# Down products of two feed-forward blocks by seven block products, with the block sums on GpSimd

## The chip, the cores and the metric

The kernel runs on one core of a Trainium2 chip. The metric is the device time of one launch in microseconds (us). The engines are TensorE (PE: matmuls, and PEld: its weight loads), VectorE (DVE), ScalarE (ACT), GpSimd (POOL) and SyncE (SP), which issues the DMAs. Each engine takes its instructions in the order in which they stand in its own queue and waits at semaphores for the others.

## What is computed

Two transformer layers over x of 4 batches x 256 positions x 256 features, all in f32:

```python
x = x + _L0_attn_ref(_layernorm(x), q_kernel, kv_kernel, out_kernel, q_norm_scale, k_norm_scale)
x = x + _L0_ffn_ref(_layernorm(x), w_gate, w_up, w_down)
x = x + _L1_attn_ref(_layernorm(x), W_K, W_Q, W_V, W_O)
x = x + _L1_ffn_ref(_layernorm(x), W1, W2, W3)
```

The change touches the two feed-forward blocks, here FFN0 and FFN1:

```python
# FFN0 (hidden size 1024)
h = silu(x @ w_gate) * (x @ w_up)
h_sparse = h * mask          # of each four neighbours the two largest by absolute value
out = h_sparse @ w_down      # 1024 -> 256
# FFN1 (hidden size 1024)
hidden = fwht(silu(x @ W1.T) * (x @ W3.T))   # Walsh-Hadamard transform along the hidden axis
out = hidden @ W2.T                          # 1024 -> 256
```

## The kernel before

**Stages.** The kernel runs attention 0 (`attention0`), FFN0 (`ffn0`), attention 1 (`attention1`) and FFN1 (`ffn1`). x stays in SBUF for the whole time, as eight tiles `xs` of 128 positions x 256 features, two per batch. A tile framework orders the instructions: it takes the program as written, estimates when each instruction could run and fixes an order for each engine when the program is built. Buffers come from pools of tagged tiles; a tag with n buffers hands them out in turn, and who gets one waits for the readers of the tile that had it before. `page` is a tag of eight 4 KB pages; the pool `late` (attention 1 and both FFNs) has the tags `qk` (2 buffers), `v` (3) and `u` (4), among others.

**FFN0.** The loop `for n in range(8)` goes over batch b = n // 2 and half gc = n % 2 of the hidden features. One step does this:
- `gated`: for w_gate, then w_up, 8 matmuls of 128x256 into a PSUM tile `pgu` (two such tiles exist: one for gate, one for up, reused in each step). ScalarE makes s = silu(gate), VectorE h = up * s (L557).
- ScalarE makes a = |h| (L530), and VectorE keeps two of four in h (`keep_two_of_four`: three comparisons at L569, 8 small sums in bf16 at L581 and L582, 4 products at L583). The positions are arranged so that the four neighbours lie in four different planes of h.
- `normed(.., by_dma=True)` at some steps: the layer norm of a later batch, whose transposition goes over a GpSimd copy (`xpl`, L240), a DMA and a ScalarE copy (`xnT`, L195).
- For n >= 2, `down(hs, n - 2, down_sb)`: the down product of two steps before, 2 position tiles x 4 matmuls of 128x256 into two PSUM tiles `po_f`. When the second half of a batch has been added, VectorE adds each `po_f` to `xs` (L604).

The down products of n = 6 and 7 are left for `finish_ffn0`, which attention 1 calls in its first step.

**Attention 1.** A software pipeline of project, score and attend over 16 units (head group, batch). Its projections use seven block products instead of eight already (`seven_products`, with sums of blocks from `left_of` for activations and `right_of` for weights, on VectorE). A unit's scores are exponentiated on ScalarE (L226), scaled on GpSimd (`p`, L234), split into 16-bit planes on GpSimd (`pl`, L240), transposed by DMA (`plT`), joined again by VectorE and ScalarE copies (`pT`, L260) and multiplied with the values on TensorE (`av`). Towards its end the Hadamard transform is applied to the weights W2 instead of to the hidden features: matmuls with a 128x128 Hadamard matrix, then 12 GpSimd additions and subtractions of 128x512 (L830).

**FFN1.** Again 8 steps; `gated1` makes gate and up of one half by `seven_products` and h from them (L873 on ScalarE, L874 on VectorE). Into the gaps between its products it pulls pieces of the iterator `between`, here the down product of the step before, `down(hs, n - 1, w2h[0], last=True)`, which adds to `xs` and sends finished rows of the output by DMA.

Of the kernel before, what the change touches and what calls it, by code (L numbers as in the profile page):

```python
# [11 lines left out]


# [1 line left out]

# [5 lines left out]
F32 = mybir.dt.float32  # L21
# [3 lines left out]
ALU = mybir.AluOpType  # L25
AX = mybir.AxisListType

P = 128
B, T, D = 4, 256, 256
NT = T // P  # L30
# [18 lines left out]
def two_layers(ctx, tc, consts, tables, x, wq, wkv, wo, w_gate, w_up, w_down,  # L49
               w_k, w_q, w_v, w_o, w1, w3, w2, out):  # L50
    nc = tc.nc
# [21 lines left out]
    def wide(name):  # L73
        return ps2.tile([P, 2, 512], F32, tag="wide", name=name)

    def bank(shape, name):
        return ps1.tile([P, *shape], F32, tag="bank", name=name)

    def page(name):

        return work.tile([P, 4, T], F32, tag="page", name=name, bufs=8)
# [11 lines left out]
    xs = [xpool.tile([P, D], F32, tag=f"x{t}", name=f"x{t}") for t in range(B * NT)]  # L93
# [11 lines left out]
    def load_ffn(src, shape, name):  # L105
        t = fpool.tile([P, *shape], F32, tag="fw", name=name)
        nc.sync.dma_start(t, src)
        return t
# [21 lines left out]
    down_sb = load_ffn(w_down, (NF, D), "w_down")  # L130
# [392 lines left out]

    def ffn0():
        hs, xn = {}, dict(enumerate(xn_f))
        for n in range(8):
            b, gc = divmod(n, 2)
            hs[n] = h = gated(xn[b], gate_sb, up_sb, 4 * gc, "h")
            a = page("a")
            nc.scalar.activation(a, h, AF.Abs)  # L530
            keep_two_of_four(a, h)
            if gc == 0 and b + 2 < B:
                xn[b + 2] = normed(b + 2, by_dma=True)
            if n >= 2:
                run(down(hs, n - 2, down_sb))
            if n == 4:
                xn1[0] = normed(0, by_dma=True)
            if n == 6:
                xn1[1] = normed(1, by_dma=True)
                left1[0] = left_of(xn1[0])  # L540
        return lambda: run(*(down(hs, n, down_sb) for n in (6, 7)))

    def gated(xnT, w_g, w_u, f0, name):

        ps = []
        for w in (w_g, w_u):
            o = wide("pgu").rearrange("p two (f t) -> p (two f) t", t=T)
            for j in range(4):
                for c in range(NC):
                    nc.tensor.matmul(  # L550
                        o[:, j, :], lhsT=w[:, c, f0 + j, :], rhs=xnT[:, c, :],
                        start=(c == 0), stop=(c == NC - 1),
                    )
            ps.append(o)
        s, h = page("s"), page(name)
        nc.scalar.activation(s, ps[0], AF.Silu)
        nc.vector.tensor_tensor(h, ps[1], s, ALU.mult)  # L557
        return h

    def keep_two_of_four(a, h):  # L560

        c = []
        counts = work.tile([P, 8, T], BF16, tag="page", name="counts", bufs=8)
        for i in range(3):
            n = 3 - i
            ci = counts[:, (0, 3, 5)[i] : (3, 5, 6)[i], :]
            nc.vector.tensor_tensor(  # L569
                ci, a[:, i : i + 1, :].to_broadcast([P, n, T]), a[:, i + 1 :, :], ALU.is_ge  # L570
            )
            c.append({i + 1 + k: ci[:, k, :] for k in range(n)})
        sums = (
            (c[0][1], ALU.add, c[0][2], ALU.add, c[0][3], 2.0, ALU.is_ge),
            (c[1][2], ALU.add, c[1][3], ALU.subtract, c[0][1], 1.0, ALU.is_ge),
            (c[2][3], ALU.subtract, c[0][2], ALU.subtract, c[1][2], 0.0, ALU.is_ge),
            (c[0][3], ALU.add, c[1][3], ALU.add, c[2][3], 1.0, ALU.is_le),
        )
        for j, (u, op0, v, op1, w, bound, keep) in enumerate(sums):
            n = counts[:, 6 + j % 2, :]  # L580
            nc.vector.tensor_tensor(n, u, v, op0)  # L581
            nc.vector.tensor_tensor(n, n, w, op1)  # L582
            nc.vector.scalar_tensor_tensor(h[:, j, :], n, bound, h[:, j, :], keep, ALU.mult)  # L583
# [3 lines left out]
    def down(hs, n, w, last=False):  # L587


        b, gc = divmod(n, 2)  # L590
        if gc == 0:
            pos[b] = [bank([D], "po_f") for _ in range(NT)]
        for t in range(NT):
            for j in range(4):
                nc.tensor.matmul(  # L595
                    pos[b][t], lhsT=hs[n][:, j, t * P : (t + 1) * P],
                    rhs=w[:, 4 * gc + j, :], start=(gc == 0 and j == 0),
                    stop=(gc == 1 and j == 3),
                )
                if j == 1:  # L600
                    yield
            if gc == 1:
                x = xs[b * NT + t]
                nc.vector.tensor_tensor(x, pos[b][t], x, ALU.add)  # L604
                if last:
                    at = (b * NT + t) * P
                    nc.sync.dma_start(out[at : at + P, :], x)
            yield

    def run(*generators):  # L610
        for g in generators:
            for _ in g:
                pass
# [9 lines left out]
    def left_of(xnT):  # L623

        s = late.tile([P, 4, P], F32, tag="xs4", name="xs4", bufs=4)
        x11, x12, x21, x22 = (xnT[:, c, t * P : (t + 1) * P] for t in range(2) for c in range(2))
        for i, a, b, op in (
            (0, x21, x22, ALU.add), (1, s[:, 0], x11, ALU.subtract),
            (2, x11, x21, ALU.subtract), (3, x12, s[:, 1], ALU.subtract),
        ):  # L630
            nc.vector.tensor_tensor(s[:, i], a, b, op)
        return x11, x12, s[:, 3], x22, s[:, 0], s[:, 1], s[:, 2]

    def right_of(w11, w12, w21, w22, t):

        for i, a, b, op in (
            (0, w12, w11, ALU.subtract), (1, w22, t[0], ALU.subtract),
            (2, w22, w12, ALU.subtract), (3, w21, t[1], ALU.subtract),
        ):
            nc.vector.tensor_tensor(t[i], a, b, op)  # L640
        return w11, w21, w22, t[3], t[0], t[1], t[2]

    def seven_products(product, x, z, y, c11, c12, c21, c22, shape, z_alone=True):
# [208 lines left out]
    def gated1(x, r, last, between):  # L852

        def product(o, i, first):
            for j in range(4):
                nc.tensor.matmul(  # L858
                    o[:, j, :], lhsT=r[j // 2][i - 1][:, j % 2, :], rhs=x[i - 1],
                    start=(first and j == 0), stop=True, skip_group_check=True,  # L860
                )

        gu = late.tile([P, 2, 4, T], F32, tag="qk", name="gu")
        c = gu.rearrange("p k (a m) (t c) -> p (k a) m t c", m=2, t=NT)
        for i, _ in enumerate(seven_products(
            product, st([P, 4, P], "gu_x"), bank([4, P], "gu_z"), st([P, 4, P], "gu_y"),
            *(c[:, :, m, t, :] for t in range(2) for m in range(2)), [P, 4, P],
        )):
            for _ in range({3: 1, 5: 2}.get(i, 0)):
                next(between, None)  # L870
        s, h = page("s"), page("h1")
        for t in (slice(0, P), slice(P, T)) if last else (slice(0, T),):
            nc.scalar.activation(s[:, :, t], gu[:, 0, :, t], AF.Silu)  # L873
            nc.vector.tensor_tensor(h[:, :, t], gu[:, 1, :, t], s[:, :, t], ALU.mult)  # L874
        return h

    def ffn1():
        hs, left = {}, {0: left_of(xn_f[0])}
        for n in range(9):
            if n < 8:  # L880
                b, half = divmod(n, 2)
                before = down(hs, n - 1, w2h[0], last=True) if n else iter(())
                hs[n] = gated1(left[b], r_ffn1[half], n == 7, before)
                run(before)
                if n == 0:
                    xn = {1: normed(1)}
                if half == 1 and b + 2 < B:
                    xn[b + 2] = normed(b + 2, by_dma=True)
                if half == 0 and b + 1 < B:
                    left[b + 1] = left_of(xn[b + 1])  # L890
            else:
                run(down(hs, n - 1, w2h[0], last=True))

    xn_f, xn1, left1, w2h, r_ffn1 = [], {}, {}, [], []
# [5 lines left out]
    late = ctx.enter_context(  # L900
        tc.tile_pool(name="late", bufs=2, reuse_waits="tile", side="right")
    )
    load_group1(0)
    load_group1(1)

    finish_ffn0 = ffn0()
    xn_f.clear()
    ps2_open.close()
    w1_sb = load_ffn(w1, (NC, NF, P), "w1")
    w3_sb = load_ffn(w3, (NC, NF, P), "w3")  # L910
    w2_raw = load_ffn(w2, (NF, D), "w2")
    st_open, st_pool = open_pool("st", bufs=4, space=PSUM)
    attention1(finish_ffn0)
    ffn1()
    st_open.close()

# [81 lines left out]
```

## Time and profile before

Three runs took 738.60, 738.98 and 739.04 us, a median of 738.98. The profiled execution has a span of 737.2 us; the traces' times are counted from the start of that span. The page gives no other time of that execution; what a run holds around its span is the 1.8 us between the two.

| stretch of the profiled execution, us | what runs | PE busy | DVE busy | ACT busy | POOL busy |
|---|---|---|---|---|---|
| 0 to 278.8 | attention 0 | 271.24 | 215.66 | 192.44 | 204.57 |
| 278.8 to 371.7 | FFN0 and the first projection of attention 1 | 92.47 | 71.94 | 25.92 | 11.17 |
| 371.7 to 655.0 | attention 1 | 282.11 | 146.33 | 157.30 | 125.51 |
| 655.0 to 737.2 | FFN1 | 79.17 | 35.21 | 31.27 | 3.79 |

How to read the profile: busy time is the union of an engine's instructions in a stretch. An instruction's row has its source line (L557), its engine, what it writes and reads, the shape of one instruction, and how often. Matmuls overlap in a pipeline: the time between the starts of two is their pace, while the length of one (0.38 us for 128x256) also holds its way through the array. A matmul of f32 in the code shows as two records. A timeline row is: start, length from the first start to the last end of the group, engine, line, operation, how often, and in brackets the engine's idle time just before it with what ended it. Another view gives all instructions of one line, with the shortest, median and longest in ns.

### The profile page before, as it was taken

To read this page: it belongs to the slowest core of one execution; us is meant where nothing else is said; L and a number is where in the kernel's file an instruction comes from. 1 tells how busy PE (TensorE), PEld (TensorE's weight loads), DVE (VectorE), ACT (ScalarE), POOL (GpSimd) and SP (SyncE) were. 2 spreads that over 40 slices of the span, in tenths; PEclk is the share of its full clock that TensorE was granted. 3 is DMA by queue.
4 is the path that set the end of the run, shared out by engine and by line. 5 is a ranking of instruction groups with operands and counts; after the bars stand their busy time and mean duration, and the time that the engine had idled before them with its cause. 6 is when DMAs were issued, how large, how long until landed. Compare 5 with 4: busy or idle time off the path is not lost.

```text
span 737.2 us, 11593 instructions
## 1 busy us (share of the span) xinstructions
PE 725.0 (98%) x3912; PEld 594.6 (81%) x3912; DVE 469.2 (64%) x1402; ACT 406.9 (55%) x983; POOL 345.0 (47%) x489
## 2 busy tenths in 40 slices
PE   9999999999999999999999999999999999999998
PEld 5556576666666778888898999999998999899997
DVE  6999878888887537987655644464442655464443
ACT  2487887667767952222355555555556576434332
POOL 1588878897799631011116433343336575520000
PEclk9999999999999999999999999999999999999999
DMA  8732344425445545001324532342232223401100
GB/s 327 293 64 51 57 93 81 92 52 93 90 79 96 77 114 180 16 14 26 119 72 77 127 55 44 70 129 46 44 72 44 44 44 44 88 15 22 23 14 30
DMA packets 138348, 57.51 MB, mean 78 GB/s; under 512 B 131504, under 2 KB 133680, under 8 KB 137520
## 3 DMA queue, kind: packets, MB, share of 16 engines
q1 hardware_dynamic: 138288, 56.77, 33.9%
q8 instruction: 31, 0.51, 0.3%
q14 instruction: 29, 0.24, 0.1%
HBM read 22.94 MB, written 1.05 MB: 33 GB/s over the span
## 4 chain that ended last, share of the span: by engine, by line
PE 75%; DVE 9%; POOL 7%; issue 4%; ACT 3%; DMA 2%; SPq 0%; POOLq 0%; DVEq 0%; ACTq 0%
PE pj L446 10%; PE pgu L550 7%; PE po L292 7%; PE po_f L595 7%; PE qk_x L783 5%; PE po L280 5%; PE sc L214 5%; PE gu_x L858 4%; PE av L394 3%; PE qk_y L783 3%; PE v_x L789 3%; PE sc L213 3%; PE av L268 2%; POOL p L234 2%; PE gu_y L858 2%
## 5 line engine op out<-in xcount | busy, mean ns | idle before, releaser
L234 POOL TENSOR_SCALAR p<-p,rs 128x128 f32<-128x128 f32 (+1 forms) x256 | 115.4, 470 | 153.2 <-DVE rs L231 147.9
L240 POOL TENSOR_SCALAR pl<-p 128x1536 uint16<-128x1536 uint16 x64 | 94.3, 1474 | 4.8 <-POOL p L234 0.5
L260 ACT COPY pT<-plT 128x1536 uint16<-128x1536 uint16 (+1 forms) x60 | 86.2, 1494 | 11.5 <-DMA plT<-pl 11.5
L216 DVE CUSTOM_DVE_ANT_0 p<-sc,cst 128x128 f32<-128x128 f32 (+1 forms) x256 | 79.7, 351 | 10.5 <-PE sc L214 8.1
L226 ACT ACTIVATE p<-p,nb,r 128x128 f32<-128x128 f32 (+1 forms) x128 | 68.2, 535 | 20.2 <-DVE nb L223 20.2
L446 PE MATMUL pj<-wq,xnT 128*128 128x512 f32 x128 | 61.1, 595 | 1.1 <-DVE qT L508 1.1
L446 PE MATMUL pj<-wkv,xnT 128*128 128x512 f32 x128 | 60.1, 592 | 0.0
L226 ACT ACTIVATE p<-p,nb 128x128 f32<-128x128 f32 (+1 forms) x128 | 56.3, 447 | 4.0 <-DVE nb L221 4.0
L292 PE MATMUL po<-wo,zT 128*128 128x256 f32 x256 | 57.9, 379 | 0.0
L280 PE MATMUL po<-w_o,zT 128*128 128x256 f32 x256 | 57.6, 379 | 0.0
L456 ACT ACTIVATE sq<-pj 128x512 f32<-128x512 f32 (+1 forms) x64 | 30.9, 489 | 42.7 <-DVE qc L451 42.4
L292 PEld LDWEIGHTS po<-wo,zT 128*128 128x128 f32 x256 | 48.3, 190 | 7.0 <-ACT kT L519 0.6
L280 PEld LDWEIGHTS po<-w_o,zT 128*128 128x128 f32 x256 | 47.7, 190 | 6.0
L156 POOL TENSOR_SCALAR ve<-mv 128x2 f32<-128x2 f32 (+1 forms) x17 | 4.3, 253 | 97.5 <-DVE mv L152 97.0
L446 PEld LDWEIGHTS pj<-wkv,xnT 128*128 128x128 f32 x128 | 24.3, 190 | 30.2 <-issue 28.0
L451 DVE TENSOR_TENSOR qs<-pj,sin_s 128x512 f32<-128x512 f32 (+1 forms) x64 | 35.3, 551 | 13.5 <-PE pj L446 12.9
L446 PEld LDWEIGHTS pj<-wq,xnT 128*128 128x128 f32 x128 | 23.5, 190 | 24.2 <-issue 19.9
L666 ACT COPY qk<-qk_x 128x512 f32<-128x512 f32 x16 | 9.4, 587 | 58.1 <-PE qk_x L783 58.1
L268 PE MATMUL av<-pT,v 128*128 128x256 f32 x128 | 38.4, 382 | 1.2 <-DVE nb L221 1.1
L214 PE MATMUL sc<-kT,qT 128*128 128x256 f32 x128 | 38.3, 381 | 0.0
L214 PE MATMUL sc<-qk 128*128 128x256 f32 x128 | 38.2, 380 | 0.0
L240 POOL TENSOR_SCALAR qpl<-qc 128x1024 uint16<-128x1024 uint16 x20 | 28.8, 1453 | 18.9 <-PE av L398 8.2
(151 smaller groups left out, 1748.8 us busy)
## 6 DMA issues: line engine op xcount, KB each, us to landing
w<-in_w_dram SPq DMA_DIRECT2D x3, 1024.0 KB, 4.7
wq<-in_wq_dram SPq DMA_DIRECT2D x4, 512.0 KB, 7.6
wkv<-in_wkv_dram SPq DMA_DIRECT2D x4, 512.0 KB, 8.4
wo<-in_wo_dram SPq DMA_DIRECT2D x4, 512.0 KB, 10.2
w_qk<-in_w_q_dram SPq DMA_DIRECT2D x4, 512.0 KB, 5.2
w_qk<-in_w_k_dram SPq DMA_DIRECT2D x4, 512.0 KB, 6.1
w_v<-in_w_v_dram SPq DMA_DIRECT2D x4, 512.0 KB, 7.3
w_o<-in_w_o_dram SPq DMA_DIRECT2D x4, 512.0 KB, 6.0
```

The lines of the kernel that those rows point to most:

```text
L214: nc.tensor.matmul(sc[:, P : 3 * P], lhsT=q[:, P:T], rhs=k, start=True, stop=True)
L216: last_of["mx"] = nc.vector.tensor_tensor_reduce(out=p[:, j, cols], in0=sc[:, cols], in1=mask[:, cols], scale=1.0, scalar=-3.0e38, op0=ALU ...
L226: last_of["exp"] = nc.scalar.activation(p[:, j, cols], p[:, j, cols], AF.Exp, bias=nb[:, j, i : i + 1], scale=SCALE1 if rq is None else rq ...
L234: nc.gpsimd.tensor_scalar(p[:, j, cols], p[:, j, cols], rs[:, j, i : i + 1], 1.0, ALU.mult, ALU.mult)
L240: last_of["planes"] = nc.gpsimd.tensor_scalar(o, i, 1.0, 1.0, ALU.mult, ALU.mult)
L260: copy(words.rearrange("p (n w) -> p w n", w=2), halves[:, :, js].rearrange("p w j n -> p w (j n)"),)
L268: nc.tensor.matmul(av, lhsT=v0, rhs=pT[:, 0:T], start=True, stop=False, skip_group_check=True)
L280: nc.tensor.matmul(po[:, t, :], lhsT=zT[:, j, t * P : (t + 1) * P], rhs=w[:, j, :], start=(t == j == 0), stop=(j == 3), skip_group_check=True,
L292: nc.tensor.matmul(po, lhsT=zTs[hd // 4][:, hd % 4, t * P : (t + 1) * P], rhs=w[:, hd, :], start=(hd == 0), stop=(hd == n - 1),)
L446: last_of[0] = nc.tensor.matmul(pj, lhsT=xnT[:, c, t * P : (t + 1) * P], rhs=w[:, g, c, :], start=(c == 0), stop=(c == NC - 1),)
L550: nc.tensor.matmul(o[:, j, :], lhsT=w[:, c, f0 + j, :], rhs=xnT[:, c, :], start=(c == 0), stop=(c == NC - 1),)
L783: last_of[1] = nc.tensor.matmul(o[:, j, :], lhsT=wqk[i - 1][:, j // 2, j % 2, :], rhs=x[i - 1], start=(first and j == 0), stop=True, skip_ ...
```

## The change

In both FFNs the down products of the first three batches are made by seven block products instead of eight; the fourth batch keeps `down`. For one batch, h is cut into two tiles of positions and two halves of hidden features, the weights into two halves of hidden features and two of output features. Four sums of blocks of h (`left_of_down`) and four of the weights (`right_of_down`), each 128x512 f32, are made on GpSimd. `down_by_seven` has three 128x128 slices x, y and z of one PSUM tile `po_s`. Each product is 4 matmuls of 128x128 into a slice; after each, VectorE adds the slice to a quarter of the batch's rows of `xs` (L658 after the change). x serves for products 1, 6, 7 and 4 in turn, accumulating, y for 5 and 3, z for 2.

In FFN0 a batch's seven products are made a batch later: four of them in the second step of the next batch and three in the step after (all seven of batch 2 in step 7). In FFN1 they are pulled between the products of the next batch's two steps, and step 7 also pulls the first half of the last batch's down product. The weights' sums of FFN0 take a buffer of tag `qk`, those of FFN1 the space of the raw W2. The sums of h take buffers of `u` or `qk` in FFN0 and of `v` in FFN1; a and s of FFN0 move from `page` to `v`.

```diff
     def ffn0():
         hs, xn = {}, dict(enumerate(xn_f))
+        blocks = late.tile([P, 4, 4, P], F32, tag="qk", name="down_t")
+        right = right_of_down(down_sb, [blocks[:, i] for i in range(4)])
+        left, by_seven = {}, {}
         for n in range(8):
             b, gc = divmod(n, 2)
             hs[n] = h = gated(xn[b], gate_sb, up_sb, 4 * gc, "h")
-            a = page("a")
+            a = late.tile([P, 4, T], F32, tag="v", name="a", bufs=3)
             nc.scalar.activation(a, h, AF.Abs)
             keep_two_of_four(a, h)
             if gc == 0 and b + 2 < B:
                 xn[b + 2] = normed(b + 2, by_dma=True)
-            if n >= 2:
-                run(down(hs, n - 2, down_sb))
+            if gc == 1 and b + 1 < B:
...
+                left[b] = left_of_down(hs[n - 1], hs[n], s)
+            if gc == 1 and b >= 1:
+                by_seven[b - 1] = down_by_seven(left[b - 1], right, b - 1)
+                fill(by_seven[b - 1], 4 if b + 1 < B else 7)
+            elif b >= 2:
+                run(by_seven[b - 2])
...
+    def left_of_down(h0, h1, s):
+        x11, x12, x21, x22 = (h[:, :, t * P : (t + 1) * P] for t in range(2) for h in (h0, h1))
+        for i, a, b, op in (
+            (0, x21, x22, ALU.add), (1, s[0], x11, ALU.subtract),
+            (2, x11, x21, ALU.subtract), (3, x12, s[1], ALU.subtract),
+        ):
+            nc.gpsimd.tensor_tensor(s[i], a, b, op)
+        return x11, x12, s[3], x22, s[0], s[1], s[2]
+
+    def right_of_down(w, t):
+        return right_of(
+            *(w[:, 4 * k : 4 * k + 4, m * P : (m + 1) * P] for k in range(2) for m in range(2)),
+            t, nc.gpsimd,
+        )
+
+    def down_by_seven(left, right, b, last=False):
+        sums = bank([3, P], "po_s")
+        x, y, z = (sums[:, i, :] for i in range(3))
+        for o, i, t, m in (
+            (y, 5, 1, 1), (x, 1, 0, 0), (z, 2, 0, 0), (x, 6, 0, 1), (y, 3, 0, 1), (x, 7, 1, 1),
+            (x, 4, 1, 0),
+        ):
+            for j in range(4):
+                nc.tensor.matmul(
+                    o, lhsT=left[i - 1][:, j, :], rhs=right[i - 1][:, j, :],
+                    start=(i == 5 and j == 0), stop=(j == 3), skip_group_check=True,
+                )
+            to = xs[b * NT + t][:, m * P : (m + 1) * P]
+            nc.vector.tensor_tensor(to, o, to, ALU.add)
+            yield
+        if last:
+            for t in range(b * NT, b * NT + NT):
+                nc.sync.dma_start(out[t * P : (t + 1) * P, :], xs[t])
+        yield
...
     def ffn1():
         hs, left = {}, {0: left_of(xn_f[0])}
+        blocks = w2_raw.rearrange("p f d -> p (f d)").rearrange("p (i f d) -> p i f d", i=4, f=4)
+        right = right_of_down(w2h[0], [blocks[:, i] for i in range(4)])
+        h_left = {}
         for n in range(9):
             if n < 8:
                 b, half = divmod(n, 2)
-                before = down(hs, n - 1, w2h[0], last=True) if n else iter(())
+                if half == 0 and b:
+                    by_seven = down_by_seven(h_left[b - 1], right, b - 1, last=True)
+                before = iter(())
+                if n == 7:
+                    before = chain(by_seven, down(hs, 6, w2h[0]))
+                elif n >= 2:
+                    before = by_seven if half else islice(by_seven, 4)
                 hs[n] = gated1(left[b], r_ffn1[half], n == 7, before)
                 run(before)
+                if half == 1 and b + 1 < B:
...
+                    h_left[b] = left_of_down(hs[n - 1], hs[n], [t[:, i] for t in s for i in range(2)])
```

`right_of` gets a parameter for its engine, VectorE as before for the other callers.

More of the change, by code (lines that the diff above doesn't have):

```diff
@@ L14 @@
 from contextlib import ExitStack, nullcontext
+from itertools import chain, islice
 import concourse.bass as bass
@@ L533, in ffn0 @@
                 xn[b + 2] = normed(b + 2, by_dma=True)
-            if n >= 2:
-                run(down(hs, n - 2, down_sb))
+            if gc == 1 and b + 1 < B:
+                if b == 1:
+                    s = late.tile([P, 4, 4, P], F32, tag="qk", name="hsum")
+                    s = [s[:, i] for i in range(4)]
+                else:
+                    s = [
+                        late.tile([P, 4, P], F32, tag="u", name="hsum", bufs=4) for _ in range(4)
+                    ]
+                left[b] = left_of_down(hs[n - 1], hs[n], s)
[4 more added lines that the diff above has]
+                run(by_seven[b - 2])
             if n == 4:
@@ L554, in gated @@
             ps.append(o)
-        s, h = page("s"), page(name)
+        s, h = late.tile([P, 4, T], F32, tag="v", name="s", bufs=3), page(name)
         nc.scalar.activation(s, ps[0], AF.Silu)
@@ L608, in down, with fill @@
             yield
+    def left_of_down(h0, h1, s):
[30 more added lines that the diff above has]
+        yield
+    def fill(generator, n):
+        for _ in range(n):
+            next(generator, None)
     def run(*generators):
@@ L632, in left_of, with right_of @@
         return x11, x12, s[:, 3], x22, s[:, 0], s[:, 1], s[:, 2]
-    def right_of(w11, w12, w21, w22, t):
+    def right_of(w11, w12, w21, w22, t, engine=nc.vector):
         for i, a, b, op in (
@@ L639, in right_of @@
         ):
-            nc.vector.tensor_tensor(t[i], a, b, op)
+            engine.tensor_tensor(t[i], a, b, op)
         return w11, w21, w22, t[3], t[0], t[1], t[2]
@@ L881, in ffn1 @@
                 b, half = divmod(n, 2)
-                before = down(hs, n - 1, w2h[0], last=True) if n else iter(())
+                if half == 0 and b:
[5 more added lines that the diff above has]
+                    before = by_seven if half else islice(by_seven, 4)
                 hs[n] = gated1(left[b], r_ffn1[half], n == 7, before)
                 run(before)
+                if half == 1 and b + 1 < B:
+                    s = [
+                        late.tile([P, 2, 4, P], F32, tag="v", name="hsum", bufs=3)
+                        for _ in range(2)
+                    ]
+                    h_left[b] = left_of_down(hs[n - 1], hs[n], [t[:, i] for t in s for i in range(2)])
                 if n == 0:
```

## The prediction

> **What bounds the kernel now.** I read first the busy times of the page, then the busy times by stage, then TensorE's own timeline in the two FFNs, then those of the engines that feed it. The first view gives each engine's busy time and instructions, the second the same by stage.
>
> ```profile
> PE 725.0 (98%) x3912; PEld 594.6 (81%) x3912; DVE 469.2 (64%) x1402; ACT 406.9 (55%) x983; POOL 345.0 (47%) x489
> 278.80:371.70 92.90, 92.47 (x456) 81.82 (x456) 71.94 (x190) 25.92 (x34) 11.17 (x18) 1.00 0.21 62
> 655.00:737.20 82.20, 79.17 (x581) 75.06 (x580) 35.21 (x63) 31.27 (x47) 3.79 (x7) 1.00 0.08 20
> ```
>
> TensorE (the first pair of a stage row) has no room: 92.47 of the 92.90 us of FFN0, at granted clock 1.00. VectorE is the only other busy engine there, 71.94 of 92.90; GpSimd has 11.17. So a saved matmul counts in full if TensorE stays fed, and any new wait counts in full too. Second, TensorE's timeline (start, length, instructions):
>
> ```profile
> 292.64 3.62 PE L550 MATMUL pgu<-xnT,w_gate 128*128 128x256 f32 x16
> 296.09 3.19 PE L595 MATMUL po_f<-w_down,h 128*128 128x256 f32 x14
> 299.12 3.62 PE L550 MATMUL pgu<-xnT,w_up 128*128 128x256 f32 x16
> 302.57 0.59 PE L595 MATMUL po_f<-w_down,h 128*128 128x256 f32 x2
> 303.00 3.62 PE L550 MATMUL pgu<-xnT,w_gate 128*128 128x256 f32 x16
> ...
> 692.43 1.06 PE L858 MATMUL gu_x<-xnT,w 128*128 128x128 f32 x8
> 693.32 1.06 PE L858 MATMUL gu_z<-xnT,w 128*128 128x128 f32 x8
> ```
>
> Starts give the pace, lengths overlap: 16 records of 256 columns per 3.45 us (303.00 less 299.12 and 302.57), 215.8 ns each; 8 of 128 columns per 0.89 us, 111.5 ns each. An f32 matmul in the code is two records. The po_f group at 296.09 is a filler: up(2) needs the PSUM buffer that h(1) frees, and TensorE does a down product meanwhile.
>
> **Matmuls, the gain.** A batch's down product was 2 x 8 matmuls, 32 records x 215.8 = 6.91 us. Now 7 x 4 matmuls of 128 columns, 56 x 111.5 = 6.24 us. Saved 0.66 us a batch, 4.0 us over six batches.
> A rule speaks against this: the Trainium skill ("TensorE: Matmul & The Clock Gate", Back-to-back issue gap) says that in a stream of weight load and matmul pairs the spacing falls from about 131 ns at 512 columns only to 81 ns at 128. Between them 256 columns would be some 98 ns (an estimate), a half-width matmul 0.83 of a whole one, and a batch 56 x 0.83 x 215.8 = 10.0 us, a loss of 3.1; this trace's ratio is 111.5 / 215.8 = 0.52, and I go by the trace.
>
> **The sums on GpSimd.** New: 4 sums of the weights and 4 of h per batch in each FFN, 32 sums of 128x512 f32. The same shape exists (the Hadamard adds); the view of that line gives shortest, median and longest in ns:
>
> ```profile
> L830 POOL TENSOR_TENSOR w_b<-w x8: 1264/1276/1598, 565.4 to 604.0; 128x512 f32<-128x512 f32 x8
> ```
>
> They start 1.22 us apart when alone: 4 sums are 4.9 us. GpSimd has that time, but VectorE beside it does not. VectorE's and GpSimd's timelines in FFN0:
>
> ```profile
> 301.02 0.48 DVE L581 TENSOR_TENSOR counts<-counts 128x256 bf16<-128x256 bf16 x2
> 301.43 1.31 DVE L582 TENSOR_TENSOR counts<-counts 128x256 bf16<-128x256 bf16 x2
> 302.66 0.74 DVE L583 SCALAR_TENSOR_TENSOR h<-counts,h 128x256 f32<-128x256 bf16 x2
> 303.33 0.48 DVE L581 TENSOR_TENSOR counts<-counts 128x256 bf16<-128x256 bf16 x2
> 304.81 1.21 DVE L557 TENSOR_TENSOR h<-pgu,s 128x1024 f32<-128x1024 f32 x1
> ```
>
> ```profile
> 301.25 1.35 POOL L240 TENSOR_SCALAR xpl<-xn 128x512 uint16<-128x512 uint16 x2 [17.50 <-issue]
> ```
>
> Two count operations with SBUF inputs take 1.31 us instead of 0.48 while two GpSimd copies run; each ends as a copy ends. An f32 sum, t_qk at 282.18, took 1.09 instead of 0.68 beside the copies at 281.86. Sums that read PSUM (qk<-qk_y, 0.69) are the same beside the Hadamard adds. So a GpSimd instruction holds a VectorE operation on SBUF until it ends, then they alternate. Between no hold and 1.6 us each (the longest add), I take a full 1.25 us, as these rows have it.
> The Trainium skill ("GPSIMD Engine Reference", Engine selection) says to keep elementwise sums on VectorE, where two-input ones run about twice as fast. By that rule a batch's sums would be 4 x 0.60 (t_qk's spacing) = 2.4 us of VectorE, less than the holds below.
>
> **FFN0, step by step.** The order in which the changed program's instructions stand on each engine is fixed when it is built; I follow it with the durations above, each engine taking its next instruction when its inputs are there. Times are of the profiled execution; up(n), gate(n) and h(n) are those of loop step n, P1 to P7 the block products.
> - Without fillers until the first sums exist, TensorE runs gate and up of n = 0 to 3 in a row. Gate(2) ends at 296.1; up(2) waits for h(1), which VectorE multiplies at 296.87 for 1.2 us: start 298.2, idle 2.1. The held counts of h(1) are now free (GpSimd's copy stands behind the sums), h(2) comes at 304.0, up(3) at 305.25: idle 0.15.
> - h(1) is final at 304.0 and four sums start. The product h(2) reads PSUM and Abs(2) fills 1.1 us, which hides two sums; two sums hold the three comparisons until 310.85 and two copies hold 1.3 us more. h(3) moves to 315.2 and up(4) to 316.45, where TensorE is ready at 313.95: idle 2.5.
> - P6 waits 0.45 for the add that reads P1 out of the same PSUM slice, queued behind the counts.
> - P4 writes the slice that P7 used. That add is queued on VectorE behind the whole of counts(4), itself held by the next batch's sums: P4 at 332.4 against 330.35, idle 2.05.
> - Batch 1's P4 has the same wait. Here the sums also hold the four left sums (xs) ahead of h(6): up(7) 0.3 late, P4 at 355.65 against 353.2, idle 2.45.
> - The norm for attention 1 comes later, and its copy stands on ScalarE ahead of u<-qk_y: 0.6 idle before qk's third product.
> Sum 10.6 idle, less 3 x 0.66 saved, less 0.43 (qk_x's present wait at 364.20 is gone): +8.2; followed to the next project's first matmul (371.68 before) I get 379.6, +7.9. I take +8.0. Without any hold the same walk leaves 2.1 + 1.0 + 0.3 idle, 3.4 less 2.4, +1.0; with 1.6 us holds three times four sums cost some 4 more, +12.
> VectorE's adds grow from 2 x 0.34 to 7 x 0.21 us a batch by spacing (128 of 256 columns at 0.42, 128x128 at 0.28), 0.8 each, in the walk. The weight sums cost nothing: three fall into GpSimd's 15.4 us gap before 280.22, the fourth delays t_qk by up to 1.3, as VectorE then waits 1.31 for TensorE; without that cover 1.3. VectorE's copy at 267.56 may be held by one of the three until 268.6, 1.0 late; its reader starts at 270.19, so this costs nothing, and up to 1.0 if that reader came sooner. No DMA is added, and the tiles of s and a only change pools.
>
> **Attention 1's tail.** The Hadamard weights' four sums follow the last adds on GpSimd:
>
> ```profile
> 600.01 5.62 POOL L830 TENSOR_TENSOR w_b<-w 128x512 f32<-128x512 f32 x4
> 608.05 1.63 POOL L234 TENSOR_SCALAR p<-p,rs 128x128 f32<-128x128 f32 x4 [2.43 <-DVE rs L231]
> ```
>
> ```profile
> 618.56 1.99 ACT L260 COPY pT<-plT 128x768 uint16<-128x768 uint16 x2
> ```
>
> Adds end at 605.6, sums at about 611.2, so p, due at 608.05, and its transposes are 3.15 late. ScalarE's second copy (619.5, the later of the two below) had its transposed half about 1.2 earlier, 3.7 after GpSimd's last copy at 614.4: it is 1.9 late, and the exponentials of the next unit stand behind that copy. The last two units form a chain (a normalised p, its transpose, its copy, the next scores) to the end, where TensorE already waits for a copy at 646.73. Bounds 0 and 3.2; I take +1.9.
>
> **FFN1.** Saved 2.0. VectorE is light, but each batch's first block product needs a sum: x4 ends, h is 3.1 us later, the sum 1.27 more, 4.45 in all, against four products x 0.89 = 3.57 of other work: 0.9 idle for batches 1 and 2, 0.35 for batch 0. Net +0.2; bounds -2.0 (all hidden) and +1.5 (1.6 us sums behind held ones). The outputs' DMAs only move to a batch's end; the last batch's stay.
>
> **Sum.** 8.0 + 1.9 + 0.2 = +10.1 on a span of 737.2, 747.3. The median is 738.98, 1.8 above that span, so I forecast 749.0.
>
> **Rivals.** (1) Faster: TensorE stays fed, 4.0 and 0.4 saved, 734.6. It needs less than 4.4 us of idle over both FFNs, so VectorE would have to deliver h(1), h(3) and the P7 adds some 8 us sooner in all. For it: VectorE has 20 us free in FFN0. Against: the first 2.1 need no hold at all, and up(4) hangs on counts in the very stretch where the sums run. (2) GpSimd's sums do not hold the comparisons: +1.0 + 1.9 + 0.2, 742.1. For it: no row shows L569 or L583 held. Against: L582 and t_qk. (3) VectorE becomes FFN0's bound, holds of 1.6 and late chains after it: +12 + 3.2, 754. For it: adds beside copies took 1.6. (4) The block products cost more than half a product, as if 0.6: 56 x 129 = 7.25, 0.34 a batch lost instead of 0.66 won, 755; against it, the 128-column rows in both stages.
>
> **How the numbers follow.** Main case 0.66 (746 to 752), no hold 0.12, VectorE bound 0.12, dear products 0.02, faster 0.05, and 0.03 for what falls between the first two rivals, within 0.2% of now (1.5 us, about what a measurement can tell from no change). Slower 0.92, same 0.03, faster 0.05. The range 741.5 to 754 takes in the main case and most of rivals 2 and 3.
>
> **What would show it.** TensorE idle before up(2), up(4) and before the po_s groups that write x after P7, with VectorE named as releaser; the comparisons and counts (L569 and L581 here) longer than 0.95 and 0.28 beside the sums; p's first GpSimd line after 608 about 3 us late against the adds; po_s at 111 ns a record. I am wrong if FFN0's TensorE idle stays under 4 us, or if the order in which TensorE finds its inputs hides the P7 adds.

## The result, and the profile after

The changed kernel takes 756.98 us (median of five runs, 756.37 to 758.42), the kernel before 738.97 in the same session. The ratio is 1.0249, with a 95% interval of 1.0238 to 1.0261: 18.0 us slower, where 10.1 were forecast, and outside the forecast's range.

The profiled execution of the changed kernel has a span of 755.2 us, again 1.8 under the median. Setting the same instructions of both traces side by side (the first gate product, the first qk_y of the second projection, the first gu product, the end) gives the loss by stage:

| us against before | attention 0 | FFN0 and first projection | attention 1 | FFN1 | span |
|---|---|---|---|---|---|
| forecast | 0 | +8.0 | +1.9 | +0.2 | +10.1 |
| measured | +0.2 | +10.7 | +3.6 | +3.5 | +18.0 |

The busy line of the page and the stages (FFN0, attention 1, FFN1) of the changed kernel, in the columns of the views shown of before:

```profile
PE 729.2 (97%) x4056; PEld 598.0 (79%) x4056; DVE 489.4 (65%) x1432; ACT 406.1 (54%) x983; POOL 388.0 (51%) x521
279.00:382.50 103.50, 94.20 (x527) 82.86 (x526) 82.74 (x205) 24.77 (x32) 30.80 (x31) 0.98 0.18 52
382.50:669.50 287.00, 283.44 (x1828) 260.76 (x1827) 149.32 (x539) 158.41 (x449) 130.06 (x188) 1.00 0.32 66
669.50:752.40 82.90, 79.89 (x653) 76.63 (x651) 40.74 (x78) 30.63 (x47) 19.11 (x19) 1.00 0.09 19
```

TensorE, which was busy for all but 0.4 us of FFN0, now has 9.3 us of idle there, and VectorE's busy time there went from 71.94 to 82.74. TensorE's timeline in FFN0, the rows with an idle of some length:

```profile
298.33 5.41 PE L566 MATMUL pgu<-xnT,w_up 128*128 128x256 f32 x16 [1.89 <-DVE h L573]
303.57 3.62 PE L566 MATMUL pgu<-xnT,w_gate 128*128 128x256 f32 x16
...
316.10 1.16 PE L653 MATMUL po_s<-w_down,h 128*128 128x128 f32 x8 [1.54 <-DVE x L658]
322.47 1.16 PE L653 MATMUL po_s<-w_down,h 128*128 128x128 f32 x8 [0.47 <-DVE x L658]
330.95 1.16 PE L653 MATMUL po_s<-down_t,hsum 128*128 128x128 f32 x8 [0.72 <-DVE x L658]
336.97 1.16 PE L653 MATMUL po_s<-w_down,h 128*128 128x128 f32 x8 [0.48 <-DVE x L658]
354.63 1.16 PE L653 MATMUL po_s<-down_t,hsum 128*128 128x128 f32 x8 [2.16 <-DVE x L658]
367.81 1.16 PE L842 MATMUL qk_y<-xs,w_qk 128*128 128x128 f32 x8 [1.98 <-ACT u L707]
```

Five block products wait for `x<-po_s` (L658), the add of the product before: by their order these are P1, P2 and P7 of batch 0, and P1 and P7 of batch 1. P1 waits for P5's add and P2 for P1's, though they write another slice of `po_s`. The last row waits for ScalarE's copy u. The first is up(2), late as forecast; but its 16 records then take 5.24 us to the next start instead of 3.45. The windows of 1 us around it show why in their third column from the end, the granted clock:

```profile
299.00:300.00 1.00, 1.00 (x5) 0.86 (x4) 0.60 (x1) 1.00 (x2) 0.00 (x0) 0.67 0.03 8
300.00:301.00 1.00, 1.00 (x4) 0.72 (x4) 1.00 (x3) 0.28 (x1) 0.00 (x0) 0.50 0.00 0
301.00:302.00 1.00, 1.00 (x4) 0.81 (x3) 1.00 (x5) 0.00 (x0) 0.00 (x0) 0.50 0.00 0
302.00:303.00 1.00, 1.00 (x5) 0.79 (x4) 1.00 (x5) 0.00 (x0) 0.00 (x0) 0.62 0.00 0
```

What is late ahead of P1 is on VectorE. Its timeline, and GpSimd's beside it:

```profile
299.40 1.90 DVE L585 TENSOR_TENSOR counts<-a 128x768 bf16<-128x768 f32 x3 [0.48 <-ACT a L534]
...
304.17 1.21 DVE L573 TENSOR_TENSOR h<-pgu,s 128x1024 f32<-128x1024 f32 x1
306.51 4.42 DVE L585 TENSOR_TENSOR counts<-a 128x768 bf16<-128x768 f32 x3 [1.12 <-ACT a L534]
310.85 1.31 DVE L597 TENSOR_TENSOR counts<-counts 128x256 bf16<-128x256 bf16 x2
...
314.63 1.21 DVE L573 TENSOR_TENSOR h<-pgu,s 128x1024 f32<-128x1024 f32 x1
315.77 0.27 DVE L658 TENSOR_TENSOR x<-po_s,x 128x128 f32<-128x128 f32 x1
```

```profile
304.40 1.27 POOL L633 TENSOR_TENSOR hsum<-h 128x512 f32<-128x512 f32 x1 [19.05 <-DVE h L599]
305.75 1.27 POOL L633 TENSOR_TENSOR hsum<-hsum,h 128x512 f32<-128x512 f32 x1
306.98 1.99 POOL L633 TENSOR_TENSOR hsum<-h 128x512 f32<-128x512 f32 x1
308.92 1.72 POOL L633 TENSOR_TENSOR hsum<-h,hsum 128x512 f32<-128x512 f32 x1
310.61 1.41 POOL L241 TENSOR_SCALAR xpl<-xn 128x512 uint16<-128x512 uint16 x2
```

Three comparisons take 4.42 us, where they take 1.90 with no GpSimd instruction beside them (at 299.40), and GpSimd's sums are lengthened in turn, from 1.27 to 1.99 and 1.72. The add of P5 stands behind h(3) in VectorE's queue, at 315.77, and P1 starts right after it.

In attention 1, GpSimd's weight sums (L699) stand between the Hadamard adds and the next p, with no gap:

```profile
612.35 5.29 POOL L889 TENSOR_TENSOR w_b<-w 128x512 f32<-128x512 f32 x4
617.60 2.83 POOL L699 TENSOR_TENSOR w<-w_b 128x512 f32<-128x512 f32 x2
620.38 2.62 POOL L699 TENSOR_TENSOR w<-w_b,w 128x512 f32<-128x512 f32 x2
622.98 1.62 POOL L235 TENSOR_SCALAR p<-p,rs 128x128 f32<-128x128 f32 x4
```

And in FFN1 TensorE waits three times for a first sum, and once for an add:

```profile
690.46 1.16 PE L653 MATMUL po_s<-w,hsum 128*128 128x128 f32 x8 [0.54 <-POOL hsum L633]
691.46 0.83 PE L917 MATMUL gu_x<-xnT,t_gu 128*128 128x128 f32 x6
...
696.38 1.13 PE L653 MATMUL po_s<-w,hsum 128*128 128x128 f32 x8 [0.88 <-DVE x L658]
...
709.02 1.16 PE L653 MATMUL po_s<-w,hsum 128*128 128x128 f32 x8 [0.56 <-POOL hsum L633]
...
729.37 1.16 PE L653 MATMUL po_s<-w,hsum 128*128 128x128 f32 x8 [0.55 <-POOL hsum L633]
```

A listed idle is less than a wait's price. The next start after 690.46 is 1.00 later instead of 0.89, and by the pace of the rows before it this one is 0.70 late, not 0.54. So 0.54 of listed idle costs 0.81, some 0.27 on top of the idle; the waits of FFN0 listed above, from P1 on, come out at 0.27 or 0.28 on top as well.

### The profile page after: what moved, and what is told of

Read it like the earlier page. It is cut to its first block, busy times and chain, and to the rows that moved or that the text cites. A ratio compares the mean times of both kernels' runs of the same rounds, so it can differ in the third digit from the quotient of the medians.

```text
span 755.2 us, 11958 instructions
## 1 busy us (share of the span) xinstructions
PE 729.2 (97%) x4056; PEld 598.0 (79%) x4056; DVE 489.4 (65%) x1432; ACT 406.1 (54%) x983; POOL 388.0 (51%) x521
## 4 chain that ended last, share of the span: by engine, by line
PE 63%; DVE 13%; POOL 10%; ACT 5%; DMA 4%; issue 4%; SPq 0%; POOLq 0%; DVEq 0%; ACTq 0%
PE pj L447 10%; PE po L293 7%; PE qk_x L842 5%; PE po L281 5%; PE sc L215 4%; PE po_s L653 4%; PE av L395 3%; PE gu_x L917 3%; POOL p L235 2%; PE qk_y L842 2%; PE av L269 2%; PE v_x L848 2%; PE sc L214 2%; POOL pl L241 2%; PE v_zy L848 2%
```

## The experiments

Every run was compared with the kernel before on the same chip. As the medians of before lie between 737.81 and 738.97, by chip and session, the ratio is what counts; the stage columns are lengths from one profiled execution, against those of before. Attention 0, whose code no run changes, is up to 1.5 us shorter than before in some of these executions (e3, e4 and e8, on one chip).

| run | median | ratio (95%) | FFN0 | attention 1 | FFN1 |
|---|---|---|---|---|---|
| changed kernel | 756.98 | 1.0249 (1.0238 to 1.0261) | +10.7 | +3.6 | +3.5 |
| e1 FFN0 only | 752.45 | 1.0182 (1.0166 to 1.0198) | +12.0 | +0.6 | +0.2 |
| e2 FFN1 only | 745.32 | 1.0090 (1.0075 to 1.0105) | 0.0 | +2.9 | +3.7 |
| e3 h sums on VectorE | 743.55 | 1.0078 (1.0063 to 1.0093) | +3.5 | +3.0 | -0.3 |
| e4 two PSUM tiles | 749.08 | 1.0160 (1.0145 to 1.0175) | +5.6 | +3.9 | +1.9 |
| e5 gap filled | 757.49 | 1.0266 (1.0245 to 1.0286) | +11.2 | +4.0 | +3.5 |
| e6 weight sums late | 755.81 | 1.0227 (1.0207 to 1.0246) | +12.8 | +0.9 | +3.5 |
| e7 no h sums | 745.26 | 1.0101 (1.0086 to 1.0116) | +3.1 | +4.4 | -0.2 |
| e8 FFN1, P1 first | 740.54 | 1.0038 (1.0024 to 1.0052) | 0.0 | +1.3 | +1.6 |
| e9 FFN1, VectorE's sums | 738.50 | 0.9996 (0.9987 to 1.0004) | 0.0 | +0.3 | -0.5 |
| e10 both, VectorE's sums, late weights | 742.96 | 1.0054 (1.0042 to 1.0067) | +3.2 | +1.0 | -0.3 |
| e11 as e10, gap filled | 743.06 | 1.0062 (1.0050 to 1.0075) | +2.8 | +3.5 | -0.3 |
| e12 both, batch 0 of FFN0 old | 740.19 | 1.0020 (1.0011 to 1.0029) | +0.6 | +1.2 | -0.3 |

**One half at a time (e1, e2).** e1 takes FFN1's functions from the kernel before, e2 FFN0's.

```diff
 # e1
-                    before = by_seven if half else islice(by_seven, 4)
 ...
+                before = down(hs, n - 1, w2h[0], last=True) if n else iter(())
 # e2
-                by_seven[b - 1] = down_by_seven(left[b - 1], right, b - 1)
 ...
+            if n >= 2:
+                run(down(hs, n - 2, down_sb))
```

> FFN0 as changed, FFN1 with the old down products; the weights' sums of FFN1, which stood on GpSimd in attention 1, are gone too. Theory A (the loss is made place by place, as the changed trace's offsets lie: 0.2 in attention 0, 10.7 in FFN0 and the projects after it, 0.6 at the start of attention 1, 3.0 in its tail, 3.5 in FFN1): 738.97 + 11.5 = 750.5. Rival B (the tail of attention 1 is late because all of it was pushed by FFN0, not because of the sums on GpSimd): 750.5 + 3.0 = 753.5. Rival C (my forecast's sizes): 738.97 + 8.0 = 747.0.

> FFN1 as changed, FFN0 with the old down products. Theory A: tail of attention 1 3.0 and FFN1 3.5 late, 738.97 + 6.5 = 745.5. Rival B (attention 1's tail is late only after a late FFN0): 742.5. Rival C (my forecast's sizes, 1.9 + 0.2): 741.1. The two parts together add up to the whole change if A holds: 11.5 + 6.5 = 18.0.

e2's time is theory A's to 0.2 us, +6.6, but partly by luck: of its 2.9 in attention 1 only 1.9 are lost in the tail, where A had 3.0. The other 1.0 is lost at the start, where A had nothing, and its cause shows in e9, below. The 1.9 in the tail, with FFN0's products as before, refute rival B. e1 is 2 us over A, nearer to B by its time, but its attention 1 loses 0.6 in all, 0.3 of it in the tail. In its profile FFN0 costs 12.0 instead of 10.7, with the clock at 0.50 from 355.3 on, behind batch 1's wait for P7, and not at 299 as in the changed kernel. Its four runs lie between 750.52 and 753.11, so A's 750.5 is its fastest run.

**The gap ahead of up(2) filled (e5).**

```diff
         for w in (w_g, w_u):
+            if fill_up and w is w_u:
+                spare = bank([T], "spare")
+                for _ in range(4):
+                    nc.tensor.matmul(
+                        spare, lhsT=w[:, 0, f0, :], rhs=xnT[:, 0, :], start=True, stop=True
+                    )
```

> As changed, and four f32 matmuls of 256 columns (8 records, 1.73 us at full clock), whose result nothing reads, between gate and up of FFN0's third step, where TensorE has 1.9 us of idle ahead of up(2). Theory A (the granted clock falls to 0.50 for some 3.5 us because of that idle, and costs 1.8 us): the clock stays at 1.00 and the time is 756.98 - 1.8 = 755.2, between 754.9 and 755.5. Rival B (the slow 16 records after the idle are held by something else, a load or a wait that the trace doesn't name): 757.0.

Theory A is refuted in its price. The 16 records after the gap are at full speed, yet nothing is won: P1 then waits 3.01 instead of 1.54, for the same add. It starts 37.1 us after the first gate product with the slow clock (changed kernel) and without it (e5, and e1 and e6, where the clock kept up at this place). The timelines of e5 and, without a filler but with the clock kept too, of e1:

```profile
315.42 1.26 PE L659 MATMUL po_s<-w_down,h 128*128 128x128 f32 x8 [3.01 <-DVE x L664]
```

```profile
315.58 1.16 PE L653 MATMUL po_s<-w_down,h 128*128 128x128 f32 x8 [3.02 <-DVE x L658]
```

So VectorE sets the place of P1, and the slow clock at 299 only filled time in which TensorE would have waited. In e5 the clock fell at 316 instead, behind this wait, so e5 does not price a fall on its own.

**The weight sums moved (e6).**

```diff
-        right = right_of_down(w2h[0], [blocks[:, i] for i in range(4)])
+        with tc.issue_after(last_of["planes"].ins):
+            right = right_of_down(w2h[0], [blocks[:, i] for i in range(4)])
```

> As changed, but the four sums of the Hadamard weights stand on GpSimd behind its last plane copy of attention 1 and the next norm's (about 12 us free there), so that no p of attention 1 waits for them; nothing else moves on TensorE, VectorE or ScalarE. Theory A (these 5.4 us on GpSimd make attention 1's tail 2.9 late): 756.98 - 2.9 = 754.1. Rival B (the tail is late because the Hadamard adds, now later, hold VectorE's copies of pT: 1.57 and 1.60 against 0.71 and 0.79): only 1.0 to 2.0 of it goes, 755.0 to 756.0.

By stage this is theory A: attention 1 loses 0.9 instead of 3.6, 2.7 less where 2.9 were expected. By its time alone it would be rival B, since in the profiled run FFN0 took 2.1 longer, with the clock at 0.50 twice (from 316.6 and from 367.8). The copies of pT that B names are short again here, so e6 takes both causes away at once. The four runs spread from 753.22 to 756.81. e10, below, repeats the move with less scatter.

**The sums of h on VectorE (e3), or left out (e7).**

```diff
 # e3
-            nc.gpsimd.tensor_tensor(s[i], a, b, op)
+            nc.vector.tensor_tensor(s[i], a, b, op)
 # e7
-            nc.gpsimd.tensor_tensor(s[i], a, b, op)
 ...
-        return x11, x12, s[3], x22, s[0], s[1], s[2]
+        return x11, x12, x12, x22, x21, x21, x21
```

> As changed, but the four sums of h of each batch run on VectorE in both FFNs (the weights' sums stay on GpSimd). Theory A (it is GpSimd's sums that hold VectorE: beside the first batch's four the comparisons took 4.42 instead of 1.90 and the next counts 1.31 instead of 0.48, 3.4 us, against 4 x 0.60 = 2.4 us of VectorE's own): the wait ahead of P1 and of batch 1's P7 becomes about 1 us shorter each, and in FFN1 the three waits of 0.9 for the first sum become about 0.3: 756.98 - 2 - 1.9 = 753. Rival B (2.4 us of sums ahead of the product h is as bad as the holds, and the order on VectorE gets worse): FFN0 no better or worse by 1, FFN1 -1.9: 755 to 756.

> As changed without the four sums of h of a batch, in both FFNs: where a block product takes a sum it takes a raw block of h, so the down products of three batches are left wrong; matmuls, adds and the weights' sums are all there. It shows what the sums of h cost, holds and waits together. Theory A (most of FFN0's loss is the hold on VectorE, and my walk without holds left +1.0 there): FFN0 +1 to +4 by the adds' waits that stay, attention 1 +3.6, FFN1 +3.5 - 2.7 = +0.8: 744.5 to 747.5. Rival B (the loss is the chain of product, add and product behind VectorE's counts, with or without sums): FFN0 stays near +9, 752.

Both are theory A, and e3 far beyond its size: moving twelve plus twelve sums from GpSimd to VectorE takes the ratio from 1.0249 to 1.0078, some 12.6 us of the 18.0; by stage, 7.2 in FFN0 and 3.8 in FFN1. Leaving the sums out altogether (e7) is no faster than having VectorE do them. VectorE's timeline in e3 at the place shown above:

```profile
302.92 1.21 DVE L573 TENSOR_TENSOR h<-pgu,s 128x1024 f32<-128x1024 f32 x1
304.05 0.68 DVE L633 TENSOR_TENSOR hsum<-h 128x512 f32<-128x512 f32 x1
304.76 0.69 DVE L633 TENSOR_TENSOR hsum<-hsum,h 128x512 f32<-128x512 f32 x1
305.37 0.68 DVE L633 TENSOR_TENSOR hsum<-h 128x512 f32<-128x512 f32 x1
305.98 0.69 DVE L633 TENSOR_TENSOR hsum<-h,hsum 128x512 f32<-128x512 f32 x1
306.58 1.89 DVE L585 TENSOR_TENSOR counts<-a 128x768 bf16<-128x768 f32 x3
308.38 0.49 DVE L597 TENSOR_TENSOR counts<-counts 128x256 bf16<-128x256 bf16 x2
...
311.34 1.22 DVE L573 TENSOR_TENSOR h<-pgu,s 128x1024 f32<-128x1024 f32 x1
```

From h(2) to h(3) it is 8.42 us here, 10.46 in the changed kernel and 7.10 in e7. No comparison or count is held (1.89 and 0.49 in the rows ahead of h(3)). VectorE's busy time in FFN0 is the same in e3 as in the changed kernel, 82.33 against 82.74. It is not less work: four sums of 0.61 each begin in the time in which VectorE waits 1.1 us for |h| anyway, while GpSimd's sums, which begin 0.9 us sooner after h(2), run for 6 us and hold the comparisons, and the copies behind them hold the counts, that the next h stands behind.

**x in a PSUM tile of its own (e4).**

```diff
-        sums = bank([3, P], "po_s")
-        x, y, z = (sums[:, i, :] for i in range(3))
+        x, yz = bank([P], "po_x"), bank([2, P], "po_yz")
+        y, z = yz[:, 0, :], yz[:, 1, :]
 ...
-                    start=(i == 5 and j == 0), stop=(j == 3), skip_group_check=True,
+                    start=(i in (5, 1) and j == 0), stop=(j == 3), skip_group_check=True,
```

> As changed, but x has a PSUM tile of its own, and y and z share another, in both FFNs. Theory A (with x, y and z in one tile each block product waits for the add of the one before it, whatever slice that read): these waits go where the two are in different tiles. FFN0: P1 then waits only for up(4)'s cause (h(3)), about 1.8 less, and the 0.7 ahead of P2 goes; P4 then waits for P7's add; FFN1: the 1.05 at the third product goes. 756.98 - 3.5 = 753.5. Rival B (VectorE's lateness is the limit and the wait moves to the next product or to up): 756 to 757.

Theory A, and nearly twice its size: the ratio falls to 1.0160, 6.6 us. With the sums still on GpSimd, FFN0 loses 5.6 instead of 10.7, and FFN1 1.9 instead of 3.5. The gains of e3 and e4 can't be added, as both are taken from the same waits for late adds.

**Versions with the causes taken out (e8, e9, e10, e11, e12).** e8 and e9 leave FFN0 old and begin each batch of FFN1 with products of raw blocks; the weight sums are late as in e6 (in e10, e11 and e12 too). e9, e10, e11 and e12 have VectorE's sums as in e3, and e11 the filler of e5. In e8, as in e2, the tiles a and s of FFN0 stay in the pool tag `v`; e9 also puts them back into `page`.

```diff
 # e8, e9, e12
-            (y, 5, 1, 1), (x, 1, 0, 0), (z, 2, 0, 0), (x, 6, 0, 1), (y, 3, 0, 1), (x, 7, 1, 1),
+            (x, 1, 0, 0), (z, 2, 0, 0), (y, 5, 1, 1), (x, 6, 0, 1), (y, 3, 0, 1), (x, 7, 1, 1),
 ...
 # e9
-            a = late.tile([P, 4, T], F32, tag="v", name="a", bufs=3)
+            a = page("a")
 ...
-        s, h = late.tile([P, 4, T], F32, tag="v", name="s", bufs=3), page(name)
+        s, h = page("s"), page(name)
 # e12, FFN0
+            if n in (2, 4):
+                run(down(hs, n // 2 - 1, down_sb))
```

> FFN0 with the old down products; FFN1 by block products in the order 1, 2, 5, 6, 3, 7, 4, so that the first two take raw blocks of h, and the weights' sums behind the last plane copy of attention 1. Theory A (the tail's 2.9 comes from the weights' sums, and 3 x 0.9 of FFN1's waits from the first sum): 738.7 + 6.6 - 2.7 - 2.7 = 739.9, between 739 and 741. Rival B (the wait moves to the next product, which reads a sum or waits for an add): 742.5. Rival C (all waits gone, only the matmuls saved): 737.

> The kernel before with FFN1 alone by block products: order 1, 2, 5, 6, 3, 7, 4, sums of h on VectorE, the weights' sums on GpSimd behind the last plane copy of attention 1. Theory A (what is left of FFN1's loss are adds held by GpSimd's sums of h): no wait of over 0.3 us on a block product, the matmuls' 3 x 0.66 saved less some 0.5 for small waits: 1.5 us faster than before. Rival B (VectorE's own adds and sums delay the products of gate and up): no faster than before, 0 to +1.

> As changed, with the sums of h on VectorE in both FFNs and the weights' sums of FFN1 on GpSimd behind the last plane copy of attention 1. Theory A (the two effects are independent: 743.6 - 737.8 = +5.7 with VectorE's sums, of which attention 1's tail is 2.0): 1.7 less, +4.0 on before. Rival B (the tail is late for VectorE's sake): +5.5.

> As the run before this one (VectorE's sums, late weights' sums), and the four spare matmuls between gate and up of FFN0's third step. There VectorE no longer holds up the product that follows. Theory A (the fall of the granted clock after that idle costs 1.8 us where nothing behind it waits anyway; where the first block product waited 3.0 it hid the fall): 1.8 less than the run before this one. Rival B (the fall comes whatever stands there, or moves to another place): no difference, within 0.5.

> VectorE's sums of h, late weights' sums, order 1, 2, 5, 6, 3, 7, 4, and batch 0 of FFN0 by the old down product, whose matmuls fill the gap ahead of up(2); batches 1 and 2 of FFN0 and three of FFN1 by block products. Theory A: against +4.0, 2.05 of idle and 1.8 of clock go and 0.66 of saved matmuls are given up: +0.8 on before, between -1 and +1.5. Rival B (the five batches' 3.3 us of matmuls are nearly all kept): -2.

e8's 740.54 lies at the top of A's range, but its chip's before is 0.9 faster than the 738.7 that A started from. By the ratio it loses 2.8 us, where A had 1.2 and at most 2.3 and B had 3.8: between the two. The waits for sums are gone, but P5 or P6 still waits for an add twice (listed idle 0.91 and 0.55), and VectorE's sums in e9 take that away too. e9 then has no wait of over 0.3 us in FFN1 and should have won 1.5. It is equal to before, as rival B had it: the interval allows a gain of 1.0 us at most. In its trace FFN1 is 0.5 shorter: 2.0 saved, and 1.9 lost in sixteen delays of 0.1 to 0.2 at changes between products, where before lost 0.4 in four. Its attention 1 loses 0.3, where e8 loses 1.3: the 1.0 at the start, which e2 has too, is gone with a and s back in `page` (the engine of FFN1's sums, the only other difference between the two kernels, comes into play later). e10 is A (+4.0). e11's time is rival B's, but e10's profiled run has the idle of 1.89 without a fall of the clock, so there was nothing for the filler to win there, and VectorE sets the next starts anyway:

```profile
297.72 3.72 PE L566 MATMUL pgu<-xnT,w_up 128*128 128x256 f32 x16 [1.89 <-DVE h L573]
305.26 3.72 PE L566 MATMUL pgu<-xnT,w_up 128*128 128x256 f32 x16 [0.36 <-DVE h L573]
313.69 1.13 PE L566 MATMUL pgu<-xnT,w_up 128*128 128x256 f32 x4 [0.36 <-DVE h L573]
```

The +3.5 of e11 in attention 1 belongs to its profiled run, the longest of the five: one transposing DMA landed after 5.6 us instead of 3.7, and the clock fell behind that wait. e12 is at the upper end of A, still 0.2% slower than before. No version beat the kernel before. Two PSUM tiles together with VectorE's sums were not tried.

## Why the prediction was wrong, and what of it held

The direction, the three places and the hold of GpSimd's sums on VectorE held. The sum was 7.9 us short: 2.7 in FFN0, 1.7 in attention 1, 3.3 in FFN1 and 0.2 ahead of them. By its own steps:

**Matmuls.** Right. Eight records of 128 columns go in 0.89 us in the block products too (309.97 to 310.87 in e4), and FFN1 of e9 is 0.5 shorter with 1.5 more lost in small delays, as a saving of 2.0 leaves it. Rival 4 is out, and with it the issue-gap rule that I had weighed.

**The sums hold VectorE.** Right, and with what waits for the sums themselves the largest cost: 12.6 of the 18.0 go with the sums to VectorE (e3). In FFN0, where no wait is put down to a sum, its 7.2 are the price of the hold; in FFN1 three waits are for a sum. The rule of the Trainium skill ("GPSIMD Engine Reference", Engine selection) that I had set beside it, elementwise sums belong on VectorE, was the better plan: 0.68 each there against 1.27 on GpSimd, and 12.6 us in the time. I had priced it at 2.4 us a batch and left it as a remark. The rule behind the hold also stands in the Trainium skill ("SBUF — State Buffer", SBUF: two separate sides): an operation of VectorE with two SBUF inputs and a GpSimd operation share a port pair that one of them has for a whole instruction. The rows above agree (4.42 for 1.90, and 1.99 for 1.27 on the other side).

**The step that failed: FFN0's chain of adds.** "P6 waits 0.45 for the add that reads P1 out of the same PSUM slice": in my walk only a product that writes a slice waited for the add that reads that slice. But x, y and z are one PSUM tile, and in the built program each product waits for the add of the one before it, in whatever slice. So the stall that I had put on up(4) already came at P1, and P2, P7 and the next batch's P1 had waits of their own. e4, which takes x out of that tile, is 6.6 us faster: 5.1 of it in FFN0, 1.6 in FFN1. Place by place, as starts that came late:

| FFN0, us | forecast | measured |
|---|---|---|
| up(2) | 2.1 | 2.05 |
| up(3), and the slow clock after up(2) | 0.15 | 1.79 |
| up(4); it came at P1 | 2.5 | 1.81 |
| P6; it came at P2 | 0.45 | 0.74 |
| P4 of batch 0; it came at P7 | 2.05 | 0.99 |
| P1 of batch 1, P2 of batch 2 | 0 | 1.10 |
| up(7) and P4 of batch 1; at P7 | 2.75 | 2.44 |
| third product of qk_y | 0.6 | 2.25 |
| small ones | 0 | 0.25 |
| sum | 10.6 | 13.4 |

The 13.4, less the 1.98 saved and the 0.70 that before loses at its own wait at 364.20 (I had taken its listed 0.43), are the +10.7. The slow clock and P1 belong together, 3.6: e5 shows that P1 would have waited that long in any case. e4 comes near what I had assumed and loses 5.6 in FFN0, not 8.0: so my walk seems to have overpriced the late counts, and the missing chain more than made up for that. The wait of qk_y had the right cause (the norm's copy stands ahead of u on ScalarE, and waits for a DMA that lands at 366.0), but the norm stands behind the late adds, and the wait cost 1.65 more than I had it.

**Attention 1: +1.9 became +3.6.** The place was right: e6 takes 2.7 of it away with the weight sums alone. The same instructions of both traces side by side, split 200 us into the stage, ahead of the late p, give its start and its tail:

| us against before | changed | e1 | e2 | e3 | e4 | e5 | e6 | e7 | e8 | e9 | e10 | e11 | e12 |
|---|---|---|---|---|---|---|---|---|---|---|---|---|---|
| start | +0.6 | +0.3 | +1.0 | +1.0 | +0.2 | +0.1 | +0.6 | +1.5 | +1.0 | 0.0 | +0.9 | 0.0 | +0.1 |
| tail | +3.0 | +0.3 | +1.9 | +2.0 | +3.7 | +3.9 | +0.3 | +2.9 | +0.3 | +0.3 | +0.1 | +3.5 | +1.1 |

With the weight sums in their place the tail loses the forecast's 1.9 in e2 and 2.0 in e3; with them moved or gone (e1, e6, e8, e9, e10) it loses 0.1 to 0.3. In the changed kernel, 0.65 of the 3.0 are a wait that e2 and e3 don't have. It stands behind VectorE's copies of pT, held in their new place beside the Hadamard adds (1.57 and 1.60 us; 0.69 and 0.81 in e6, 0.70 to 0.80 in e2 and e3). I had not counted that. VectorE and TensorE in the changed kernel, then VectorE in e6:

```profile
616.50 1.60 DVE L261 COPY pT<-plT 128x768 uint16<-128x768 uint16 x1 [0.68 <-DMA plT<-pl]
618.77 0.67 PE L269 MATMUL av<-pT,v 128*128 128x256 f32 x2 [0.32 <-DVE mx L217]
```

```profile
616.80 0.81 DVE L261 COPY pT<-plT 128x768 uint16<-128x768 uint16 x1 [0.23 <-DMA plT<-pl]
```

What is left of the 3.0, some 0.4, stays open. The longer tails of e4, e5, e7, e11 and e12 have a transposing DMA in the tail that landed after 4.5 to 5.6 us instead of 3.7. Which one is late differs between executions, and the kernel before has one of 5.2 near 610, so this is a reading of single profiles and not shown as the cause. The 0.6 at the start has no shown cause in the changed kernel. A VectorE that is late out of FFN0 may add to it, but e2 and e8, whose FFN0 has the old products, lose 1.0 there, and e9 nothing with a and s back in `page`. So the term that the prediction put at nothing, "the tiles of s and a only change pools", can alone cost 1.0.

**FFN1: +0.2 became +3.5.** The waits for the first sum were nearly right, 0.81, 0.93 and 0.93 against 0.35, 0.9 and 0.9. The premise "VectorE is light" failed: GpSimd's sums hold it here as well (a pair of sums of xs took 1.58 at 693.51, and 0.48 in the kernel before), so P6 waited 1.12 for the add of P2, in another slice of the same tile, and some 1.5 went in small delays. In e4 P6 does not wait. With VectorE's sums the stage is 0.3 shorter than before.

**Rivals.** Rival 3 (VectorE becomes FFN0's bound, 754) was the nearest, by place and by number. Rivals 1 and 2 are refuted by the 9.3 us of idle and by the 4.42.

## What to carry to other kernels

Ask of an added operation not only how long it takes on its own engine, but which instructions beside it it holds, and what stands behind those: work put on an idle GpSimd cost VectorE as much busy time as if VectorE had done it, at a worse moment. Take the dependencies between slices from the built program, as one PSUM tile for several accumulators made a chain of product, add and product here. A saving of 0.66 us a batch on a TensorE that is busy to 99% is gone with a handful of waits, each of which cost some 0.27 more here than its listed idle. Moving a tile to another pool is a change too: it went with 1.0 us here.

## What the runs showed of the hardware

The granted clock falls to 0.50 for about 3.4 us (the windows above lose 0.33 + 0.50 + 0.50 + 0.38 = 1.7 us) after some of TensorE's idles of 1.9 to 3.0 us: in the changed kernel after the idle of 1.89 at 298 and not after those of 1.54, 2.16 and 1.98; in e1 after the 2.16 and not after 1.89 and 3.02; in e10 after none in FFN0. The kernel before, e2, e7, e8, e9 and e12 have no such idle and no fall.

Which idle it is follows from the traces. In the record of the granted clock that each trace holds, the eight falls of these runs (the drop at the end of the work aside) come 86, 102, 85, 86, 91, 91, 106 and 189 stretches of 3.413 us after the first full clock (changed kernel, e1, e3, e4, e5, e6 twice, e11), whole numbers to 0.001. An idle that lies across the end of such a stretch counts in two parts. The idle of 3.02 in e1 had 1.81 ahead of an end at 314.38 and 1.20 behind it, and nothing fell; the 3.01 of e5 and e6 had 2.49 and 2.43 in one stretch, and the clock fell at its end. All eight falls close a stretch with 1.89 us of idle or more. No stretch with up to 1.81 has one, nor has one stretch with 1.91 (e5, ending at 367.54), so the bound lies near 1.9, by ends of matmuls that the profile models. The phase of the stretches differs between executions, and with it what the same idle costs.

The Trainium skill ("TensorE: Matmul & The Clock Gate", What's actually happening) has the two rates and a window of 3.4 us that runs freely, which agrees with these lengths and with the grid. Its advice to avoid gaps of over some 3 us (Why this matters for your kernels) is too mild for these runs, where 1.89 us in one stretch was enough.

In the changed kernel the fall at 299 cost nothing, since the next product waited for VectorE in any case. With falls elsewhere FFN0 is 0.5 us longer than there in e5, 1.3 in e1 and 2.1 in e6, which has two. The scatter of the changed kernels' runs goes with it: the two longest runs of the changed kernel (757.75 and 758.42) have a mean granted clock of 0.993 against 0.997 and 0.998 in the others, and the longest of e4 (751.27) and e5 (760.17) 0.995 and 0.993 against 0.998.
